# Two bottleneck layers on one core: the order of the four matmuls in a group of the projections and the last convolutions

## The chip, the core and the metric

The kernel runs on one core of one Trainium2 chip. A core has TensorE (matrix products, written to the PSUM memory), VectorE and ScalarE (elementwise work), GpSimd and SyncE (here mostly issuing DMAs), and 16 DMA engines. The metric is the device time of one execution in microseconds (us). A lower time is better.

## What is computed

Two layers on an input x of 16 images, 1024 channels, 32 x 32 pixels, all in fp32. The first is a bottleneck with local self-attention, the second a bottleneck with a 3x3 convolution:

```python
# layer 0
residual = x
h = relu(bn(conv1x1(x, w_conv1)))                 # 1024 -> 256 channels
q = relu(bn(conv1x1(h, wq))); k = relu(bn(conv1x1(h, wk))); v = bn(conv1x1(h, wv))
kp = unfold3x3(k) + (pos_h + pos_w)               # 32 heads of 8 channels, 9 taps
attn = softmax(einsum('bgdhw,bgdkhw->bgkhw', q, kp), over the 9 taps)
h = relu(bn(einsum('bgdkhw,bgkhw->bgdhw', unfold3x3(v), attn)))
x = relu(bn(conv1x1(h, w_conv3)) + residual)      # 256 -> 1024 channels
# layer 1
out = relu(bn(conv1x1(x, w1)))                    # 1024 -> 256
out = relu(bn(conv3x3(out, w2)))
x = relu(bn(conv1x1(out, w3)) + x)                # 256 -> 1024
```

## The kernel before

The channels are cut into blocks of 128 (P), so 1024 channels are NC = 8 blocks and 256 channels are NW = 2. An image has HW = 1024 pixels; a matmul of the program takes 512 of them, a half (`halves`, L308). A PSUM tile `ps` is 128 x 1024 fp32, two banks of 512 columns, one for each half; there are four such tiles, handed round.

The work of TensorE is a list of stages, one per image and kind, written out by hand (L975 to L979). `P3` stands for three stages of image 3, C, Q and V; letters stand for:

- C, the first convolution (`first_conv`, L1028): for each of 8 input blocks `reduce_part` (L352) adds four matmuls at L358 into two PSUM tiles. ScalarE then makes h, with one instruction for each of the two channel blocks (L1037).
- Q and V, the projections (`project`, L444). For each block of output channels, `conv` (L448) issues four matmuls at L454: two halves of the pixels by two input blocks of h. The order is k block 0, q block 0, q block 1, k block 1, then a product with the positions (L492), then v block 0 and v block 1. ScalarE reads each result (L466) once all four matmuls are done.
- F, the fused stage (`fused`, L1065). For each of 8 output blocks `Expand.products` (L386) issues four matmuls at L390 from the attention output a, and `reduce_part` takes the result at once into the second layer's first convolution (L358). The residual block s is put into the PSUM tile ahead by ScalarE (`seed`, L379 to L381), and `result` (L401, L417) reads the sum.
- W, the 3x3 convolution of four images in Winograd form (L771).
- U, the last 1x1 convolution (`last_sum`, L1106), again through `Expand.products`, from y.

The list puts a Q directly behind a C for thirteen images: 0 to 8, 10, 11, 13 and 14. Images 9, 12 and 15 have a U or a V in between or in front.

The attention itself (softmax over taps, weighted sums) is VectorE's, with two exps on ScalarE (L613). It takes q, k and v from DRAM in another layout and leaves the weighted sum `acc` (L631 to L651). A DMA stores that (L653), two DMAs fetch it back as the two channel blocks of a (L667), and ScalarE applies the norm and relu to each block (`finish_attended`, L670, instructions at L675).

[...] A planner in the program (`class Side`, L868) decides, while the program is built, between which steps of TensorE the pieces of attention and the exps are put, from fixed costs such as CHUNK = 3.43 (L436). DMAs are issued on three queues: loads of x, s and r and stores of results on GpSimd's, weights, the k and v stores and a on SyncE's, a few on ScalarE's.

The lines that matter are L388 to L397, L452 to L460, L356 to L364 (the inner order of the convolution into 256 channels, untouched), L381, L417, L466, L492, L1037 and L675.

Of the kernel before, what the change touches and what calls it, by code (L numbers as in the profile page):

```python
# [18 lines left out]
NW = WID // P  # L19
# [53 lines left out]
def sa_bottleneck_kernel(ctx: ExitStack, tc: tile.TileContext, x, w1t, wqkvt, w3t, u1t, u2t, u3t, params, out):  # L73
# [59 lines left out]
    def done_with(key):  # L133

        if last_use[key] == now[0]:
            more_weights()
# [3 lines left out]
    def col(name, j, n=1):  # L140
        return par[:, _COL[name] + j : _COL[name] + j + n]
# [160 lines left out]
    def inside(t, n):  # L302
        return t[:, n, 1 : 1 + H, 1 : 1 + W]

    def rows(ap):
        return ap.rearrange("p (r w) -> p r w", w=W)

    def halves(half):  # L308
        return slice(half * HALF, (half + 1) * HALF)
# [39 lines left out]
    def piece(name, half):  # L349
        return name, owner[now[0], name, half], half  # L350
# [20 lines left out]
    class Expand:  # L371
# [13 lines left out]

        def products(self, o):  # L386
            key = piece(self.name, o * 2 // NC)
            for half in range(2):  # L388
                for n in range(NW):
                    nc.tensor.matmul(  # L390
                        self.ahead[o][:, halves(half)],
                        pieces[key][:, n, o % (NC // 2) * P :][:, :P],
                        self.src[:, n, halves(half)],
                        start=False,
                        stop=(n == NW - 1),
                        skip_group_check=True,
                    )  # L397
            if o % (NC // 2) == NC // 2 - 1:
                done_with(key)
# [38 lines left out]
    def by_quarter(name, b, width, per):  # L438


        t = dram.tile([NJ, NW, P * per // HEAD_DIM, width], F32, tag=f"{name}{b}", name=name)
        return t.rearrange("j n c w -> n c j w"), t.rearrange("j n (g d) w -> (j n g) (d w)", d=per)

    def project(b):  # L444

        h = hidden.pop(b)

        def conv(which, n):  # L448
            ps = psum.tile([P, HW], F32, tag="ps", name="ps")
            name, at = ("wqk", which * WID) if which < 2 else ("wv", 0)  # L450
            key, at = piece(name, 0), at + n * P
            for half in range(2):  # L452
                for m in range(NW):
                    nc.tensor.matmul(  # L454
                        ps[:, halves(half)],
                        pieces[key][:, m, at : at + P],
                        h[:, m, halves(half)],
                        start=(m == 0),
                        stop=(m == NW - 1),
                    )  # L460
            if n == NW - 1 and which:
                done_with(key)
            return ps

        def norm(dst, src, name, n, func):
            nc.scalar.activation(  # L466
                dst, src, func,
                bias=col(f"L0_conv_{name}_b", n), scale=col(f"L0_conv_{name}_s", n),
            )

        def halo(name, which, func):

            room, backs[name] = by_quarter(name, b, HALO, HEAD_DIM)
            for n in range(NW):
                norm(inside(kp, n), rows(conv(which, n)), name, n, func)

                block = kp[:, n]
                nc.sync.dma_start(
                    room[n], AP(block.tensor, block.offset, [block.ap[0], [JROWS * PW, NJ], [1, HALO]])
                )  # L480
                yield CHUNK

        backs = relaid[b] = {}
        q = hpool.tile([P, NW, HW], F32, tag="h", name=f"q_{b}")
        room, backs["q"] = by_quarter("q", b, JPIX, HEAD_DIM)

        def positions():

            ps = psum.tile([P, HW], F32, tag="ps", name="ps")
            for half in range(2):  # L490
                for n in range(NW):
                    nc.tensor.matmul(  # L492
                        ps[n * G * NPOS : (n + 1) * G * NPOS, halves(half)],
                        pos[:, n].rearrange("p g t -> p (g t)"),
                        q[:, n, halves(half)],
                        start=True,
                        stop=True,
                    )
            by_offset = zpool.tile([P, HW], F32, tag="z", name="by_offset")
            nc.scalar.activation(by_offset, ps, AF.Identity)  # L500

            room, backs["pos"] = by_quarter("pos", b, JPIX, NPOS)
            by_offset = by_offset.rearrange("p (j w) -> p j w", j=NJ)
            for n in range(NW):
                nc.gpsimd.dma_start(room[n], by_offset[n * G * NPOS : (n + 1) * G * NPOS])

        k = halo("bnk", 1, RELU)
        yield next(k)
        for n in range(NW):
            norm(q[:, n, :], conv(0, n), "bnq", n, RELU)  # L510
            nc.gpsimd.dma_start(room[n], q[:, n, :].rearrange("p (j w) -> p j w", j=NJ))
            yield CHUNK
        yield next(k)
        positions()
        side.add(b)
        written.add(("qk", b))
        relay("qk", b)
        yield 2.5
        for n, cost in enumerate(halo("bnv", 2, AF.Identity)):
            if n:  # L520
                written.add(("v", b))
                relay("v", b)
            yield cost
# [11 lines left out]
    def relay(what, b):  # L535

        if not ((what, b) in written and (what, b) in room_for):
            return
        moved, backs = projected.setdefault(b, {}), relaid[b]
        if what == "qk":  # L540
            shapes = (("q", "qc", [HEAD_DIM, JPIX]), ("bnk", "bnk", [HEAD_DIM, HALO]), ("pos", "pc", [NPOS, JPIX]))
        else:
            shapes = (("bnv", "bnv", [HEAD_DIM, HALO]),)
        def move(name, tag, shape):
            t = apool.tile([P] + shape, F32, tag=tag, name=f"{tag}_{b}")
            nc.gpsimd.dma_start(t.rearrange("p d w -> p (d w)"), backs[name])
            moved[name] = t.rearrange("p d (r w) -> p d r w", w=PW) if shape[1] == HALO else t
            if len(moved) in (3, 4):
                come[what, b] = max(side.vector, side.tensor) if b else side.tensor

        for i, shape in enumerate(shapes):
            if b < 2 or i == 0:
                move(*shape)
            else:

                moves.append((side.tensor + GAP * i, lambda shape=shape: move(*shape)))
# [190 lines left out]
    def winograd_conv(b):  # L747
# [93 lines left out]
        for one, two in ROWS:  # L841
            for part in range(3):
                for i in (one, two):
                    products(i, part)
                    if part == 0:
                        copied(i, ones, 2.0)
                    elif part == 1:
                        copied(i, twos, 1.0)
                        side.other(along(i))
                        if i == 0:  # L850

                            middle(3, 0, 4.0)
                            side.other(6.0)
                    else:
                        side.other(last(i))
                    yield CHUNK + 0.3
# [379 lines left out]
```

## Time and profile before

| | before |
|---|---|
| median of 8 runs | 2415.78 us (2413.3 to 2418.47) |
| profiled execution, its own time | 2415.5 us |
| span of the profiled execution | 2413.7 us |
| TensorE matmul busy | 2382.8 us (99%), 6144 records |
| TensorE weight load busy | 1149.5 us (48%), 6144 records |
| VectorE busy | 2080.1 us (86%) |
| ScalarE busy | 919.4 us (38%) |
| GpSimd busy | 466.1 us (19%) |
| DMA | 691.04 MB, mean 286 GB/s |
| mean granted TensorE clock | 0.998 |

The profile is of one execution. Its span is counted from the first to the last instruction, and the execution's own time is 1.8 us more. "Busy" of the matmuls counts overlapping records once, and since a matmul's end overlaps the next one's start, the pitch from one start to the next says more than the duration of one. The profile's lines name the source line (L390), the engine (PE is the matmul, PEld the weight load, DVE is VectorE, ACT is ScalarE), the operation, output and inputs, the shape, and how often (x1024). What stands in brackets, or behind the last bar, is the time for which the engine had been idle before, and what ended that wait.

### The profile page before, as it was taken

The page shows a single profiled execution, that of the slowest core. Times are in us where ns is not written, and L with a number is a line of the kernel's source. Part 1 is how long each engine was busy: PE and PEld are TensorE (multiplying, and loading weights), DVE is VectorE, ACT ScalarE, POOL GpSimd, SP SyncE. Part 2 cuts the span into 40 slices and gives each one's busy share as a digit, 9 for nine tenths or more (in the row PEclk, how much of TensorE's full clock was granted, in tenths as well). Part 3 has the DMA queues.
Part 4 walks back from the last instruction along what each step waited for, and adds up shares of the span by engine and source line. Part 5 has one row for each costly group of instructions (what it writes and reads, how often), then busy time and mean ns, then how long its engine had stood idle before and what let it go on. Part 6 is the DMA issues. An engine that isn't in the chain of part 4 may idle for free.

```text
span 2413.7 us, 18460 instructions
## 1 busy us (share of the span) xinstructions
PE 2382.8 (99%) x6144; PEld 1149.5 (48%) x6144; DVE 2080.1 (86%) x1648; ACT 919.4 (38%) x889; POOL 466.1 (19%) x854
## 2 busy tenths in 40 slices
PE   8999999999999999999999999999999999989999
PEld 3444444444476444444476444444466444434844
DVE  4899999999999999998999999989989999873700
ACT  3323241323122574432122574334122553344265
POOL 2111111111111232111111232111111221112132
PEclk9999999999999999999999999999999999999999
DMA  9968685888798897777898997787798986788886
GB/s 357 365 209 309 246 297 211 262 294 264 267 327 273 322 395 290 237 262 242 240 312 294 298 409 273 251 283 261 243 321 302 319 327 227 241 283 271 321 297 252
DMA packets 296126, 691.04 MB, mean 286 GB/s; under 512 B 20064, under 2 KB 166496, under 8 KB 287584
## 3 DMA queue, kind: packets, MB, share of 16 engines
q0 software_dynamic: 119024, 471.40, 54.1%
q1 hardware_dynamic: 175568, 213.97, 28.0%
q10 hardware_dynamic: 1440, 4.51, 0.5%
q8 instruction: 49, 0.80, 0.1%
q14 instruction: 45, 0.37, 0.0%
HBM read 416.09 MB, written 273.70 MB: 286 GB/s over the span
## 4 chain that ended last, share of the span: by engine, by line
PE 84%; DVE 5%; DMA 4%; issue 4%; ACT 1%; POOL 1%; SPq 0%; POOLq 0%; ACTq 0%; DVEq 0%
PE ps L358 34%; PE ps L390 29%; PE ps L454 11%; PE ps L771 9%; DVE acc L631 2%; DVE acc L649 1%; PE ps L492 1%; DMA a<-a 1%; DMA U<-uw 1%; POOL out_dram L418 1%; DMA a<-acc 1%; POOL r L340 1%; ACT h L1037 1%; DMA uw<-u 0%; DMA v<-v 0%
## 5 line engine op out<-in xcount | busy, mean ns | idle before, releaser
L390 PE MATMUL ps<-a,w 128*128 128x512 f32 x1024 | 461.1, 595 | 7.2 <-ACT a L675 7.2
L358 PE MATMUL ps<-result,u 128*128 128x512 f32 x1024 | 458.4, 592 | 2.0 <-ACT result L417 2.0
L358 PE MATMUL ps<-x,w 128*128 128x512 f32 x1024 | 445.1, 595 | 6.5 <-DMA x<-in_x_dram 6.5
L390 PE MATMUL ps<-y,u 128*128 128x512 f32 x1024 | 441.2, 592 | 1.0 <-ACT ps L381 1.0
L631 DVE TENSOR_TENSOR acc<-e,bnv 128x2048 f32<-128x2048 f32 x144 | 327.5, 2283 | 36.6 <-ACT e L613 33.6
L574 DVE TENSOR_TENSOR prod<-qc,bnk 128x2048 f32<-128x2048 f32 x144 | 324.0, 2287 | 1.7
L417 ACT ACTIVATE result<-ps,par 128x1024 f32<-128x1024 f32 x128 | 142.5, 1113 | 463.2 <-PE ps L390 394.7
L390 PEld LDWEIGHTS ps<-a,w 128*128 128x128 f32 x1024 | 195.3, 191 | 255.0 <-issue 242.5
L358 PEld LDWEIGHTS ps<-x,w 128*128 128x128 f32 x1024 | 195.6, 191 | 252.8 <-issue 252.8
L358 PEld LDWEIGHTS ps<-result,u 128*128 128x128 f32 x1024 | 194.2, 190 | 248.3 <-issue 237.5
L390 PEld LDWEIGHTS ps<-y,u 128*128 128x128 f32 x1024 | 194.5, 190 | 245.9 <-issue 240.8
L649 DVE TENSOR_TENSOR acc<-acc 128x2048 f32<-128x2048 f32 x128 | 293.4, 2292 | 4.4
L454 PE MATMUL ps<-h,wqk 128*128 128x512 f32 x512 | 225.8, 595 | 5.7 <-ACT h L1037 5.7
L417 ACT ACTIVATE result<-ps,bn_sh 128x1024 f32<-128x1024 f32 x127 | 141.2, 1112 | 137.8 <-PE ps L390 137.5
L418 POOL DMA_DIRECT2D r<-result x128 | 68.8, 537 | 634.8 <-ACT result L417 619.3
L579 DVE TENSOR_TENSOR prod<-prod 128x2048 f32<-128x2048 f32 (+1 forms) x80 | 166.2, 2078 | 2.5
L454 PEld LDWEIGHTS ps<-h,wqk 128*128 128x128 f32 x512 | 96.2, 190 | 132.7 <-issue 110.0
L1037 ACT ACTIVATE h<-ps,par 128x1024 f32<-128x1024 f32 x32 | 38.6, 1205 | 288.1 <-PE ps L358 288.1
L381 ACT ACTIVATE ps<-r 128x1024 f32<-128x1024 f32 x128 | 130.4, 1020 | 26.3 <-DMA r<-r 18.8
L466 ACT ACTIVATE kp<-ps,par 128x1024 f32<-128x1024 f32 x64 | 77.4, 1210 | 160.2 <-PE ps L454 123.9
L381 ACT ACTIVATE ps<-s 128x1024 f32<-128x1024 f32 x128 | 131.2, 1025 | 2.5
L340 POOL DMA_DIRECT2D x<-in_x_dram x120 | 63.8, 532 | 299.9 <-PE ps L358 230.2
(317 smaller groups left out, 2296.1 us busy)
## 6 DMA issues: line engine op xcount, KB each, us to landing
s<-in_x_dram POOLq DMA_DIRECT2D x128, 512.0 KB, 6.3
r<-result POOLq DMA_DIRECT2D x128, 512.0 KB, 4.0
r<-r POOLq DMA_DIRECT2D x128, 512.0 KB, 6.3
out_dram<-result POOLq DMA_DIRECT2D x127, 512.0 KB, 6.1
x<-in_x_dram POOLq DMA_DIRECT2D x120, 512.0 KB, 5.2
v<-v SPq DMA_DIRECT2D x96, 408.0 KB, 4.7
U<-uw SPq DMA_DIRECT2D x72, 512.0 KB, 4.3
bnk<-kp SPq DMA_DIRECT2D x32, 680.0 KB, 7.7
```

The lines of the kernel that those rows point to most:

```text
L340: (nc.scalar if kind == "x" and b == 0 else nc.gpsimd).dma_start(t, src)
L358: nc.tensor.matmul(ps[n][:, halves(half)], wt[:, c % (NC // 2), n * P : (n + 1) * P], src[:, halves(half)], start=(c == first), stop=(c == ...
L381: nc.scalar.activation(ps, loaded.pop((self.kind, self.b, o)), AF.Identity)
L390: nc.tensor.matmul(self.ahead[o][:, halves(half)], pieces[key][:, n, o % (NC // 2) * P :][:, :P], self.src[:, n, halves(half)], start=Fals ...
L417: nc.scalar.activation(to_, ps, RELU, bias=self.shift(o), scale=1.0)
L418: nc.gpsimd.dma_start(to, t)
L454: nc.tensor.matmul(ps[:, halves(half)], pieces[key][:, m, at : at + P], h[:, m, halves(half)], start=(m == 0), stop=(m == NW - 1),)
L574: nc.vector.tensor_tensor(by_row(t[:, two]), by_row(qc), kc[:, :, i : i + JROWS, j : j + W], ALU.mult)
L579: nc.vector.tensor_add(u[:, :, 0:4], u[:, :, 0:4], u[:, :, 4:8])
L631: nc.vector.tensor_tensor(by_row(dst), rows(e[:, k, :]).unsqueeze(1).to_broadcast([P, HEAD_DIM, JROWS, W]), vc[:, :, i : i + JROWS, j : j ...
L649: nc.vector.tensor_add(acc, acc, t)
L771: nc.tensor.matmul(acc[i][:, at, :, n, :], pieces[key][:, m, at, n * P : (n + 1) * P], v[:, at, :, m * (TILES + TR) :][:, :, :TILES], star ...
```

## The change

In two places the two inner loops change places. `n` and `m` count the two blocks of input channels (the rows over which the products are summed), `half` the two halves of the pixels.

```diff
--- before.py
+++ after.py
@@ -385,8 +385,8 @@
         def products(self, o):
             key = piece(self.name, o * 2 // NC)
-            for half in range(2):
-                for n in range(NW):
+            for n in range(NW):
+                for half in range(2):
                     nc.tensor.matmul(
                         self.ahead[o][:, halves(half)],
                         pieces[key][:, n, o % (NC // 2) * P :][:, :P],
@@ -449,8 +449,8 @@
             ps = psum.tile([P, HW], F32, tag="ps", name="ps")
             name, at = ("wqk", which * WID) if which < 2 else ("wv", 0)
             key, at = piece(name, 0), at + n * P
-            for half in range(2):
-                for m in range(NW):
+            for m in range(NW):
+                for half in range(2):
                     nc.tensor.matmul(
                         ps[:, halves(half)],
                         pieces[key][:, m, at : at + P],
```

Before, a group of four was half 0 with blocks 0 and 1, then half 1 with blocks 0 and 1. After, it is block 0 with halves 0 and 1, then block 1 with halves 0 and 1. Two matmuls in a row then have the same weights and write different banks. The rest of the program text is the same.

## The prediction

> **What bounds the kernel now.** I read, in order, the page's busy table, the waits of TensorE, the costliest groups, and then the timeline at each wait. TensorE is 99% busy by the page (VectorE 86%), and the granted clock is full in nearly every slice. Its waits in the whole span, from the view that names who waited for whom, are few:
>
> ```profile
> PE ps L390 <- ACT a L675: 7.2, 2, 3.7
> PE ps L358 <- DMA x<-in_x_dram: 6.5, 1, 6.5
> PE ps L454 <- ACT h L1037: 5.7, 13, 0.4
> ```
>
> (total us, times, longest). The third row is the change's business, and the first in part. The groups show what a matmul costs when nothing is waited for:
>
> ```profile
> L390 PE MATMUL ps<-a,w 128*128 128x512 f32 x1024 | 461.1, 595 | 7.2 <-ACT a L675 7.2
> L358 PE MATMUL ps<-x,w 128*128 128x512 f32 x1024 | 445.1, 595 | 6.5 <-DMA x<-in_x_dram 6.5
> L358 PEld LDWEIGHTS ps<-x,w 128*128 128x128 f32 x1024 | 195.6, 191 | 252.8 <-issue 252.8
> ```
>
> Each `nc.tensor.matmul` is two records here: the first convolution issues 16 images x 8 blocks x 4 = 512, and the row counts 1024. The pitch of the records, from the chain of waits in order of time (start, us, what):
>
> ```profile
> 113.37 27.48 PE ps L358 x64
> 782.30 27.47 PE ps L390 x64
> 809.76 13.73 PE ps L454 x32
> 1163.32 13.14 PE ps L454 x30
> ```
>
> 27.48/64, 27.47/64 and 13.73/32 are all 0.429 us. So one program matmul is 0.858 us, in all three loops. TensorE is the bound, at a pitch that the order inside a group of four does not set; only its waits can be won.
>
> **The change, part by part.** It touches 2048 + 768 = 2816 records (L390 and L454). Nothing is added or removed: same matmuls, operands, helpers' order, DMAs and queues. Inside each group of four, the second and third matmul swap. [...]
>
> *Steady state: 0.* The new order keeps one stationary operand for two matmuls and alternates PSUM banks; that is exactly the inner order of L358 (its n outside, half inside). [...] L358 already repeats its weights, and shows 1024 loads for 1024 matmul records at the same 0.429 pitch. I take the row: no load goes, and a load would be worth nothing anyway, since it lies beside the matmul before it. [...] The distance from one accumulation to the next in the same bank becomes one matmul; it was none in L390 before, and is three or more in L358. Both ends run at 0.429, so I take 0 for what lies between.
>
> *The start of thirteen projections.* Where a projection follows a first convolution at once, its input h comes in two ACT instructions, one for each channel block. The timeline at image 1 (second is the duration):
>
> ```profile
> 88.33 1.20 ACT L1037 ACTIVATE h<-ps,par 128x1024 f32<-128x1024 f32 x1 [5.08 <-PE ps L358]
> ...
> 89.84 1.02 PE L454 MATMUL ps<-h,wqk 128*128 128x512 f32 x2
> 90.04 1.20 ACT L1037 ACTIVATE h<-ps,par 128x1024 f32<-128x1024 f32 x1 [0.51 <-PE ps L358]
> 91.30 1.98 PE L454 MATMUL ps<-h,wqk 128*128 128x512 f32 x4 [0.44 <-ACT h L1037]
> ```
>
> Block 0 is ready before the convolution ends; block 1 only at 90.04 + 1.20 = 91.24. The first matmul starts at 89.84, before the second ACT even begins, so the wait is on the block and not on the whole of h. The second matmul (half 0, block 1) could start at 89.84 + 0.858 = 90.70, and starts at 91.30: 0.60 lost. After such a stop the next record takes 0.697 instead of 0.592 (the maximum in the L454 rows), 0.105 more. Sum **0.705**. A cross-check: a projection of 32 records without a stop runs from 809.60 to 823.43 (13.83); this one runs from 89.84 to 104.37 (14.53), 0.70 longer.
>
> After the change the second matmul reads block 0 again. Block 1 is first read by the third, due at 89.84 + 1.716 = 91.56, 0.26 after the release at 91.30. The weight load that carries the wait would be due about 0.43 earlier, at 91.13, and so starts 0.17 late. That this is free is seen at image 0: its first L454 load starts at 36.79 where the regular step from 36.20 gives 36.63, and its matmul is at 37.05 all the same, one step after the last. So each stop goes whole, and nothing is late in its place: 13 x 0.705 = 9.2 us on TensorE.
>
> *Which of these reach the end.* The other engines' programs keep their order, so a gain is lost only where TensorE waits next for something that did not move. Image 0 (stop at 38.5): at 53.54 TensorE waits for q, behind an ACT that waits for a DMA begun at 40.94, after h; lost. Images 2 and 3 (142.1, 193.0): at 223.95 the fused stage waits 1.49 us for a result that sits behind a of image 0. That chain is VectorE's, from 144.48 on, started by an exp that follows the h of image 2 and not the stop. Lost: 1.4 us. The other **ten** (91.3, 301.3, 408.0, 458.9, 564.6, 670.4, 1163.3, 1214.2, 1597.0, 1757.7) lie in the printed chain as "h, then PE L454 x30", like the row at 1163.32 above. Behind them TensorE waits for nothing of more than 0.75 us until 2129. VectorE has finished each image's attention 37 us or more before its fused stage from image 1 to 14, and its last piece starts at 2067.05, after waiting 8.72 us for an exp behind ACT work that follows TensorE. So VectorE moves along. 10 x 0.705 = **7.05 us**. Bounds: 9.2 if all thirteen count, 3.5 if half of the ten are absorbed.
>
> *The fused stage of image 15.* Here a's two blocks arrive apart, by the timeline of TensorE:
>
> ```profile
> 2129.27 2.08 PE L390 MATMUL ps<-a,w 128*128 128x512 f32 x2 [3.50 <-ACT a L675]
> 2135.06 6.51 PE L390 MATMUL ps<-a,w 128*128 128x512 f32 x10 [3.71 <-ACT a L675]
> ```
>
> One matmul is done before the second block; with the change it is two, so two records fewer remain after 2135.06: 2 x 0.429 = **0.86 us**. The clock is half here (0.50 in each of the stretches from 2129.0 to 2139.0, 0.99 after), so this is counted at the pitch that follows. The trace cannot tell whether the busier stretch brings the clock back one window (about 3.4 us) sooner: upper end 0.86 + 1.7 = 2.6, lower end 0.86. I take the lower, since the 2129.00 to 2132.40 stretch was 2.08 us busy already and the clock stayed.
>
> In all other fused and last stages a, or y, is ready long before; there the swap does nothing: 0. The groups that wait for a seed wait at their first matmul in either order: 0.
>
> **Sum.** 7.05 + 0.86 = 7.9. The profiled execution took 2415.5 us (span 2413.7, 1.8 around it), 0.3 under the median shown: 2415.5 - 7.9 = 2407.6; against the median 2407.9. I say 2407.7.
>
> **Rivals.**
> - *The clock returns a window sooner* at 2132 or 2136: 2407.7 - 1.7 = 2406.0. For: more work in that window. Against: 2.3 us of idleness remain there. Chance 0.10.
> - *VectorE is the true bound* (86%, nines in most slices), and the gains only lengthen the wait for a at 2129: what stays is 0.86 and 2414.6. Also here: the waits do not shorten because they were tied to all of h. Against: the first matmul's start before the second ACT, and the 8.72 us of VectorE idleness ahead of its last piece. Chance 0.08.
> - *Half is absorbed*, by a longer landing on the path: a of image 15 took 15.25 us from issue to landing, and a weight piece U of the last Winograd stage 13.70 against a median of 4.3. 3.5 + 0.86 gives 2411.2; with one further 9.4 us landing it is 2417. Chance 0.13.
> - *Slower: the banks.* If returning to a bank after one other matmul breaks the stream, each of the 1408 program matmuls pays. It outweighs the gain from 7.9/1408 = 5.6 ns each; at the 0.105 us that a restarted stream pays above it is +148, hence 2556. L358's four banks speak against, and that the distance of one is nowhere in the trace, for. Chance 0.03.
> - The forecast: 0.66.
>
> 0.2% of this time, about what a measurement can tell from no change, is 4.8 us. Faster by more: 0.66 + 0.10 + 0.03 of the half case = 0.79; within: 0.17; slower: 0.04 (the banks, and 0.01 of late landings). The range 2404 to 2412.5 takes in the sooner clock, all thirteen stops, and half of them lost.
>
> **What would show it.** Right: the row "PE ps L454 <- ACT h L1037" is gone or near zero; all projections run at 32 records in 13.7; L390 and L454 keep a count of two loads and two matmuls per program matmul and 0.429; the waits at 53.5 and 223.9 are longer by 0.7 and 1.4; four records instead of two stand before the second a. Wrong: a pitch other than 0.429 in L390 or L454, the wait at 2129 longer by some 7 us, or fewer loads.

## The result and the profile after

| | before | after |
|---|---|---|
| median | 2415.98 us (32 runs, 2411.33 to 2422.71) | 2409.76 us (12 runs, 2405.85 to 2413.35) |
| ratio | | 0.9974, 95% interval 0.9967 to 0.9982 |
| profiled execution, own time | 2415.5 us | 2413.8 us |
| span | 2413.7 us | 2412.1 us |
| TensorE matmul busy, records | 2382.8 us, 6144 | 2382.2 us, 6144 |
| weight loads | 6144 | 6144 |
| mean granted clock | 0.998 | 0.996 |

The changed kernel is 6.2 us faster, with an interval of 4.3 to 8.0; 7.9 had been forecast. The profiled execution of the changed kernel is the longest of its thirteen, so its span is not the measure. What follows reads it in stretches.

The waits of TensorE after (who waited for whom: total us, times, longest):

```profile
PE ps L390 <- ACT a L675: 6.4, 2, 4.1
PE ps L358 <- DMA x<-in_x_dram: 6.2, 1, 6.2
PE ps L358 <- ACT result L417: 4.2, 1, 4.2
PE ps L492 <- ACT q L466: 2.5, 1, 2.5
PE ps L454 <- ACT by_offset L500: 2.3, 1, 2.3
```

The row of thirteen waits for h is gone altogether. Three others have grown. Before, they were:

```profile
PE ps L358 <- ACT result L417: 2.0, 2, 1.5
PE ps L492 <- ACT q L466: 0.9, 1, 0.9
PE ps L454 <- ACT by_offset L500: 0.3, 1, 0.3
```

The costliest groups after:

```profile
L390 PE MATMUL ps<-a,w 128*128 128x512 f32 x1024 | 462.7, 597 | 6.4 <-ACT a L675 6.4
L390 PEld LDWEIGHTS ps<-a,w 128*128 128x128 f32 x1024 | 195.9, 192 | 255.3 <-issue 243.3
L454 PE MATMUL ps<-h,wqk 128*128 128x512 f32 x512 | 222.3, 592 | 0.0
```

There is still one weight load for each matmul record, although every second matmul of the program in these two loops now has the weights of the one before it. The last of these rows was, before:

```profile
L454 PE MATMUL ps<-h,wqk 128*128 128x512 f32 x512 | 225.8, 595 | 5.7 <-ACT h L1037 5.7
```

So it fell by 3.5 us, with nothing idle before it. Image 1 again, in the timeline after, and, in the chain of waits, the projection that stood at 1163.32 before:

```profile
89.10 1.20 ACT L1037 ACTIVATE h<-ps,par 128x1024 f32<-128x1024 f32 x1 [5.85 <-PE ps L358]
90.61 3.60 PE L454 MATMUL ps<-h,wqk 128*128 128x512 f32 x8
90.82 1.21 ACT L1037 ACTIVATE h<-ps,par 128x1024 f32<-128x1024 f32 x1 [0.51 <-PE ps L358]
```

```profile
1162.53 13.73 PE ps L454 x32
```

The projection now runs on while the second ACT writes block 1. At 1162.53 it is one unbroken piece of 32 records at 13.73/32 = 0.429 us, where before the chain went over ACT and then 30 records.

**Where the gain went.** TensorE has the same 6144 records in the same stages in every kernel here, so the starts of the same record can be compared. Record 761, counted from 1, opens the second reduction (L358) of image 1's fused stage, some 7 us behind the wait near 330 us. Record 5371 lies just before the fused stage of image 15. Worked out from the traces of all profiled kernels that belong here (us; the labels are those of the experiments below):

| kernel | start of record 761 | 761 to 5371 | 5371 to the last |
|---|---|---|---|
| before | 337.9 | 1785.14 | 285.5 |
| e3, new order where nothing waits | 336.4 | 1785.14 | 284.6 |
| e5, last convolutions alone | 341.3 | 1785.14 | 286.2 |
| e1, images 0 to 4 alone | 339.0 | 1785.13 | 282.5 |
| e2, eight later images alone | 342.2 | 1779.50 | 286.4 |
| after | 341.2 | 1779.50 | 286.2 |
| e8, after once more | 349.1 | 1779.52 | 280.9 |
| e12, after once more | 340.2 | 1783.45 | 284.7 |
| e10, before with one store moved | 334.9 | 1785.16 | 281.6 |
| e9, after with that store moved | 335.1 | 1779.81 | 284.5 |
| e11, e9 once more | 336.9 | 1780.91 | 285.1 |

The middle column settles the main point. With the eight later stops it is 1785.13 to 1785.16 in each of these profiles, without them 1779.50 to 1779.52 in three: 5.64 us, or 0.705 for each stop. In the other three TensorE waits besides in a Winograd stage: e9 and e11 have 0.3 and 1.4 us more, e12 3.95, from one wait of 2.2 us for a weight piece U at 699 and half clock behind it. The first column shows no gain from the five early stops, the last none from image 15; both scatter by several us. They also say little about the medians: the profiled executions of after, e2, e5, e8 and e12 are the longest of their series, that of e10 the shortest.

### The profile page after: what moved, and what is told of

It is laid out like the page before. It is cut to its first block, busy times and chain, and to the rows that moved or that the text cites. A ratio compares the mean times of both kernels' runs of the same rounds, so it can differ in the third digit from the quotient of the medians.

```text
span 2412.1 us, 18460 instructions
## 1 busy us (share of the span) xinstructions
PE 2382.2 (99%) x6144; PEld 1151.7 (48%) x6144; DVE 2080.1 (86%) x1648; ACT 919.3 (38%) x889; POOL 466.1 (19%) x854
## 4 chain that ended last, share of the span: by engine, by line
PE 82%; DVE 9%; issue 4%; DMA 3%; POOL 1%; ACT 1%; POOLq 0%; ACTq 0%; SPq 0%; DVEq 0%
PE ps L358 32%; PE ps L390 29%; PE ps L454 11%; PE ps L771 10%; DVE acc L631 3%; DVE acc L649 2%; DVE prod L574 1%; PE ps L492 1%; POOL out_dram L418 1%; DMA a<-a 1%; DVE prod L579 1%; POOL r L340 1%; DMA bnk<-kp 1%; DMA uw<-u 0%; DMA U<-uw 0%
## 5 line engine op out<-in xcount | busy, mean ns | idle before, releaser
L358 PE MATMUL ps<-result,u 128*128 128x512 f32 x1024 | 459.6, 594 | 4.2 <-ACT result L417 4.2
L358 PE MATMUL ps<-x,w 128*128 128x512 f32 x1024 | 443.7, 594 | 6.2 <-DMA x<-in_x_dram 6.2
L358 PEld LDWEIGHTS ps<-x,w 128*128 128x128 f32 x1024 | 195.1, 191 | 251.5 <-issue 251.0
L358 PEld LDWEIGHTS ps<-result,u 128*128 128x128 f32 x1024 | 194.9, 190 | 250.8 <-issue 238.1
L1037 ACT ACTIVATE h<-ps,par 128x1024 f32<-128x1024 f32 x32 | 38.5, 1205 | 287.1 <-PE ps L358 287.1
L466 ACT ACTIVATE kp<-ps,par 128x1024 f32<-128x1024 f32 x64 | 77.4, 1209 | 151.2 <-PE ps L454 114.6
```

Of the source, the lines that this page charges most:

```text
L358: nc.tensor.matmul(ps[n][:, halves(half)], wt[:, c % (NC // 2), n * P : (n + 1) * P], src[:, halves(half)], start=(c == first), stop=(c == ...
```

## The experiments

Each was run in turn with the kernel before on the same chip. Unless said otherwise, an edit is to the kernel before.

**e1: the new order in the early images alone.**

```diff
-            for half in range(2):
-                for m in range(NW):
+            order = [(m, half) for m in range(NW) for half in range(2)]
+            if not (b in (0, 1, 2, 3, 4)):
+                order.sort(key=lambda at: at[1])
+            for m, half in order:
```

> The new order in the projections of images 0 to 4 alone; all else as before. All five stops at the first projection go, 3.5 us on TensorE. Theory A (gains before 330 us are lost, since what TensorE waits for at 330 hangs on VectorE, which did not move): 0 us in the median, ratio 1.0000, and the first matmul of the fused stage of image 1 that waits for a result (330.7 us before) comes within 1.5 us of its old time. Theory B (as the prediction has it, the stops of images 1 and 4 count): -1.4 us, 0.9994. Theory C (every stop counts): -3.5 us, 0.9985. If longer waits cost clock windows besides, A gives up to +3 us.

Measured: 2416.76 against 2415.0 us, ratio 1.0008 (1.0000 to 1.0016). The trace shows where the gain went in that execution. By 301 us TensorE was 3.6 us ahead of the kernel before (1.6 of it from a quicker start of that execution), and at the next wait 3.2 of them went. ScalarE, then SyncE's queue, in the timeline of e1 (two lines inserted above shift its numbers: L468 is L466 of before, L480 is L478, L738 is L736):

```profile
310.79 1.21 ACT L468 ACTIVATE kp<-ps,par 128x1024 f32<-128x1024 f32 x1 [2.23 <-PE ps L456]
...
328.04 1.21 ACT L468 ACTIVATE kp<-ps,par 128x1024 f32<-128x1024 f32 x1 [9.14 <-DMA bnk<-kp]
329.15 1.10 ACT L417 ACTIVATE result<-ps,par 128x1024 f32<-128x1024 f32 x1
```

```profile
313.74 1.40 SPq L738 DMA_DIRECT2D v<-v  x2
315.19 0.60 SPq L130 DMA_DIRECT2D w<-ws  x1
315.89 0.41 SPq L480 DMA_DIRECT2D bnk<-kp  x1
```

Block 1 of k is written by 312.0, but its store is issued only at 315.89, behind a store of Winograd data (v) on the same queue that waits for VectorE. The store lands at 328.0. Only then may ScalarE write v into the same buffer, and the result that TensorE waits for stands behind that write:

```profile
330.30 5.40 PE L358 MATMUL ps<-result,u 128*128 128x512 f32 x8 [3.76 <-ACT result L417]
```

In the kernel before the same place was:

```profile
330.70 3.93 PE L358 MATMUL ps<-result,u 128*128 128x512 f32 x8 [0.48 <-ACT result L417]
```

What TensorE waits for here hangs on VectorE and a landing, so a TensorE that comes earlier waits longer. The landing counts too: in e1 the store took 12.1 us from its issue until ScalarE went on, in the kernel before 10.9. The eight records then take 5.40 us instead of 3.93, since the clock is half from 330.5 to 333.9. Theory A, with its clock window, is the one that fits; B and C lie outside the interval of the median, which leaves no gain.

**e2: the eight later images alone.** The same edit with the images 5, 6, 7, 8, 10, 11, 13 and 14.

> The new order in the projections of images 5, 6, 7, 8, 10, 11, 13 and 14 alone; all else as before. Eight stops of 0.705 us go, all behind 330 us. Theories A, B and C: -5.6 us, 2410.3, ratio 0.9977. If VectorE were the bound behind 330 too: within 1 us of before.

Measured: 2410.84 us, 0.9984 (0.9976 to 0.9992), that is 1.9 to 5.8 us. The 5.6 lies at the upper end, and the trace shows 5.64 in the middle stretch to the hundredth. This profile also has a wait of 2.9 us at 333.5 with a half-clock window, though its code is that of before up to there. With the early stops in place that wait was 0.5 us in two profiles (before and e3), 2.9 and 4.1 in two others (e2 and e5, the longest executions of their series) and not there in e4; without them it was 3.3 to 4.2 in four (after, e1, e8, e12).

**e3: the new order wherever nothing waits.** The edit of e1 with `b in (9, 12, 15) or (which, n) != (1, 0)`, and the like in `products` with all but the fused stage of image 15.

> The new order wherever nothing is waited for: all projection groups but the first (k, block 0) of the thirteen images behind a first convolution, and all groups of the last convolutions but the fused stage of image 15. If the order costs nothing in itself: ratio 1.0000, pitch 0.429 us in L390 and L454, and the row of waits for h unchanged at 13. If the alternation of banks or the repeated weights were worth something, 2816 records less the excepted ones would show it: 1 ns a record is 2.6 us.

Measured: 2415.15 us, 0.9999 (0.9992 to 1.0006); the thirteen waits for h are there, and the middle stretch is 1785.14, as before. The order in itself is worth nothing, neither by its weights nor by its banks.

**e4: the stop made longer.** The late block first, in the first group of the thirteen:

```diff
+            late = (which, n) == (1, 0) and b not in (9, 12, 15)
             for half in range(2):
-                for m in range(NW):
+                for m in reversed(range(NW)) if late else range(NW):
...
-                        start=(m == 0),
-                        stop=(m == NW - 1),
+                        start=(m == (NW - 1 if late else 0)),
+                        stop=(m == (0 if late else NW - 1)),
```

> As before, but in the first projection group of the thirteen images the late block of h comes first (in both halves), so that the first matmul and not the second waits for it. The stop grows from 0.60 + 0.105 to 1.46 + 0.105 us, by 0.86. If eight to ten stops lie on the path to the end: +6.9 to +8.6 us, ratio 1.003. If all thirteen count: +11.2. If VectorE hides them: +1 or less.

Measured: 2425.1 us, 1.0041 (1.0028 to 1.0054), +10.1 (6.8 to 13.0). Its waits row (one line inserted above shifts the numbers):

```profile
PE ps L455 <- ACT h L1038: 16.8, 13, 1.3
```

Thirteen waits of 1.3 us. The middle stretch is 1791.98, +6.84 for eight stops, 0.855 each as computed. The rest of the +10.1 is not placed: the stretches outside the middle scatter too much, and the interval holds both eight stops and thirteen. At the eight, TensorE's time is the kernel's time, in both directions.

**e5: the last convolutions alone.** The first hunk of the change.

> The new order in the last convolutions alone (L390), projections as before. Only the fused stage of image 15 can gain: four records instead of two before the late block of a, 0.86 us, ratio 0.9996 (to -2.6 us, 0.9989, if the clock comes back a window sooner). If the longer first burst makes the clock no better and the wait takes a further window, 0 to +1 us. The thirteen waits for h stay.

Measured: 2414.56 us, 0.9995 (0.9987 to 1.0003): cannot be told from nothing, nor from the 0.86. In its trace the move happened and did not pay. In the changed kernel's it is the same:

```profile
2127.53 3.78 PE L390 MATMUL ps<-a,w 128*128 128x512 f32 x4 [4.09 <-ACT a L675]
2133.65 7.74 PE L390 MATMUL ps<-a,w 128*128 128x512 f32 x11 [2.33 <-ACT a L675]
```

Four records stand before the late block, as forecast. But the half clock holds until 2139.2, and did until 2139.0 before (13.7 us of it in the changed kernel's profile, 10.2 in the first), and how long these waits are differs by us from profile to profile (from record 5371 to the last: 281.6 to 287.1 in all profiles with the old order at this place, 280.9 to 286.2 with the new one).

**e6 and e7: all stores of k and v on ScalarE's queue.** In `halo`, on the changed kernel (e6) and on the one before (e7):

```diff
-                nc.sync.dma_start(
+                nc.scalar.dma_start(
                     room[n], AP(block.tensor, block.offset, [block.ap[0], [JROWS * PW, NJ], [1, HALO]])
```

> The changed kernel, and the stores of k and v (L478) issued by ScalarE's DMA queue instead of SyncE's, where the store of k's block 1 of image 4 stood behind a store of Winograd data that waits for VectorE (issued at 317.64, its data ready at 313.76). Theory A (the wait at 330 eats the early gains through that queue): the store goes some 3.5 us sooner, the wait of 4.2 us for the result at 332.5 falls under 1.5, no half-clock window follows it, and the median falls by 2 to 5 us under the changed kernel, to 2405 to 2408. If the landing is bound by the DMA engines and not by the issue: no change against the changed kernel. If ScalarE pays for 64 issues of about 0.4 us where TensorE waits for it: slower by a few us.

> The kernel before, with the stores of k and v on ScalarE's queue as in e6. Theory A: with that wait out of the way the order of the matmuls is worth more than before: this minus e6 is 7 to 9 us (8 stops of 0.705 behind 330, 0.7 to 2.1 ahead of it, 0.86 at image 15), and this one is within 3 us of the kernel before, since its wait at 330 was 0.5 us. If the early gains are lost elsewhere: the difference stays near 6.

Measured: 2426.55 us, 1.0043 (1.0030 to 1.0056), and 2427.11 us, 1.0045 (1.0033 to 1.0057). Both miss what was expected by far, and so does their difference: 0.6 us, where 7 to 9, or else 6, had been expected. The wait near 330 did go (in e6 the store was issued at 318.98, right behind its activation of 317.74). Others came or grew elsewhere, in e6 these:

```profile
PE ps L390 <- ACT ps L381: 5.9, 4, 2.6
PE ps L454 <- ACT by_offset L500: 5.3, 1, 5.3
PE ps L358 <- ACT result L417: 4.4, 1, 4.4
```

In two of the three ScalarE's own order shows. At by_offset ScalarE now issues the store before it (0.37 us, and 0.44 of waiting for its own write); the longer part of that wait is that the two blocks of a landed some 2.6 us later than in the changed kernel, and why was not tried. The wait for a result is at 614; on ScalarE that result (612.95) stands behind exps, the first of which had waited 12.30 us for VectorE. It is in e6 and not in e7, and with the half clock behind it puts e6 back by 7.1 us there, although each stop is still gone at its place, for 0.7 us. So in these two kernels the order does not show in the time: what was won at the stops was lost at a wait that came in one profile and not in the other.

**e8: the changed kernel again.**

> The changed kernel once more, for a second profile beside the others on one chip. All theories: ratio 0.9974 within its interval. Theory A: no wait for h, a wait for the first result near 330 again longer than the 0.5 us of before, and the eight stops behind it worth 5.6 us in the positions of TensorE's records; whether half-clock windows follow the waits at 54 and at 330 varies from run to run.

Measured: 2408.96 us, 0.9975 (0.9969 to 0.9982), 22 runs. The wait for a result was there again (3.9 near 330, 5.0 in two), and the middle stretch was 1779.52. One thing missed: there was a wait for h, of 1.2 us at 38.8. It stands before the first matmul of image 0's projection, that is, it is for the early block, so the order has no part in it. With a wait of 4.8 us for q at 60.15 it makes this profile's start the latest of the table.

**e9 and e10: one store moved.** On the changed kernel (e9) and on the one before (e10):

```diff
-                nc.sync.dma_start(
+                (nc.scalar if (name, n, b) == ("bnk", 1, 4) else nc.sync).dma_start(
```

> The changed kernel with one DMA moved: the store of k's block 1 of image 4 goes on ScalarE's queue, all 63 others stay on SyncE's. Theory A: it is issued right after its data (about 313 and not 317), the wait for the first result near 330 (4.2, 3.8 and 3.9 us in the three profiles with the early stops gone) falls under 1 us with no half-clock window of 1.4 us behind it, and the median falls 2 to 5 us under the changed kernel: 2404 to 2407, ratio to before 0.9955 to 0.9967. Theory D (the DMA engines are full there and the store lands late whatever the queue): as the changed kernel, 0.9975.

> The kernel before with that same one store on ScalarE's queue. Theory A: the wait at 330, 0.5 us in one profile of that code and 2.9 and 4.1 in two others, goes; 1 to 4 us under the kernel before. The order of the matmuls is then worth 7 to 8 us (e9 against this): 5.6 behind 330 and 1.4 ahead of it, and what image 15 gives. Theory D: as before, 1.0000, and the difference stays at 6.

Measured: e9 2406.85 us, 0.9966 (0.9954 to 0.9979); e10 2416.2 us, 1.0003 (0.9994 to 1.0011). The rows did what theory A says. In e9 the store goes at 313.85, and TensorE walks from the last convolution into the reduction without a wait:

```profile
321.33 7.03 PE L390 MATMUL ps<-a,w 128*128 128x512 f32 x16
328.19 3.60 PE L358 MATMUL ps<-result,u 128*128 128x512 f32 x8
```

Record 761 came at 335.1 and 334.9, earlier than in all the others. But e10's median did not fall, and its profile is its shortest execution, 7.6 us under that median. The medians of e9 and e10 are 9.4 us apart, where 7 to 8 had been expected, or 6; with five runs of e9 this does not tell one from the other.

**e11 and e12: e9 and the changed kernel once more, side by side.**

> e9 once more, beside the changed kernel on the same chip, to settle whether the moved store is worth anything in the median. Theory A: 2 to 4 us under e12, ratio to before 0.996 to 0.9967. Theory D: the same as e12 within 1 us.

> The changed kernel a third time, beside e11. All theories: ratio 0.9974 within its interval; in the profile no wait for h, and a wait of 3 to 5 us for the first result near 330.

Measured: e11 2409.32 us, 0.9974 (0.9964 to 0.9984); e12 2408.77 us, 0.9976 (0.9964 to 0.9988). Theory D's number: the moved store is worth nothing that can be measured, although it takes the wait at 330 away (record 761 at 336.9, no wait for a result in its list). So that wait explains the early loss in the profiles in which it stands; that it does so in the median was not shown, and what else holds the first 330 us is open. In the profile of e11 the wait just ahead of it, at 212, was 3.5 us with a half-clock window, where e12 had 1.1 and none. No version that beats the changed kernel was found.

## Why the prediction was right

*The bound and the steady state: right.* TensorE, at 0.429 us a record in either order (13.73 us for 32 records of a projection before and after; the middle stretch of e3 is that of before, 1785.14). There are 6144 loads before and after, and no half clock came with the alternating banks (0.998 granted in the mean before, 0.996 after, 0.998 in e3; in the profiles of before and after the half clock between 15 and 2300 us lies at waits or right behind them). Each record has a load of its own in every order here, so what one load for two matmuls would be worth was not tried.

*The stop of 0.705 us: right.* Thirteen of thirteen are gone in the changed kernel's profile, 0.705 each for the eight that the middle stretch measures; its lengthening by e4 was right too.

*Which stops reach the end: partly wrong.* The prediction's step was "the other ten lie in the printed chain" and "behind them TensorE waits for nothing of more than 0.75 us until 2129". The wait at 330.7, small in that profile, was passed over. It does not follow TensorE: it hangs on a store behind VectorE's on SyncE's queue, and in the profile of e1 it took what the stop at 301.3 and those ahead of it had won. None of the five early stops is seen in the median of e1. Eight count, 5.64 us, in place of ten and 7.05. Of the two waits that were to grow, the one for q at 53.5 grew by 1.6 us instead of 0.7, and the one at 223.9 went, since TensorE was already held 2.1 us longer at 212, by by_offset, which stands behind a of image 0 on ScalarE.

*Image 15: the step failed in its result.* The two records more before the late block are there, but the 0.86 us for them is seen in no median and no stretch. The wait around it varies by more.

*The sum.* The measured 4.3 to 8.0 holds both 5.6 and the forecast's 7.9, so the time alone does not show that two of the ten stops and image 15 are missing; the median's 6.2 lies nearer to eight stops. The parts run alone (e1 +1.8, e2 -4.2, e5 -0.6) add up to about -3, with some 1.9 us of uncertainty in each; that they come to less than the whole is within what such a sum can be off, and is left open.

*The rivals.* VectorE is not the bound of the middle stretch. In the profiles with a wait near 330 it is part of what holds TensorE there; the rival had placed its effect at 2129. The banks cost nothing (e3: 0.9999 of the time before). Whether the clock returns sooner at image 15 is not told apart: its half clock lasts 3.4 to 13.7 us in the profiles with the new order there, 6.8 to 13.7 in those with the old. One figure of the half case is a slip: 2417 is the forecast of 2407.6 with a 9.4 us landing; on top of 2411.2 it would be 2420.6.

## What to carry to other kernels

When an input arrives in pieces, one behind the other (here two of 1.20 us from ScalarE), order the consumer so that everything that the first piece allows comes before the first use of the second; two matmuls of cover (1.7 us) hid the rest of a 1.2 us activation thirteen times, at no cost. Before counting such gains to the end, look for the next wait of the bound engine even where it is short: what ended it tells whether it moves along, and a short one in one profile may be long in the next (near 330, 0.5 us in the profile of before, 2.9 in that of e2, whose code is the same up to there). Comparing the start of the same record in two traces, stretch by stretch, resolved hundredths of a us where the medians resolved about two us.

## What was not expected of the hardware

A short wait of TensorE can cost more than itself. With some came half clock, in the profiles of before and after for 3.41 to 13.65 us at a time, in which the records ran at 0.85 us instead of 0.43. The changed kernel's stretches near 330 (busy time of TensorE, its weight loads, VectorE, ScalarE and GpSimd, then the clock granted to TensorE, DMA share, GB/s):

```profile
324.00:328.00 4.00, 4.00 (x11) 1.56 (x9) 3.93 (x4) 0.00 (x0) 0.00 (x0) 1.00 1.05 335
328.00:332.00 4.00, 0.31 (x1) 0.00 (x0) 3.50 (x4) 1.72 (x2) 0.00 (x0) 1.00 1.15 325
332.00:336.00 4.00, 3.46 (x6) 1.39 (x7) 3.93 (x5) 3.36 (x4) 1.97 (x4) 0.70 1.08 323
336.00:340.00 4.00, 4.00 (x10) 1.81 (x9) 4.00 (x2) 0.00 (x0) 0.18 (x1) 0.88 1.09 272
```

The wait fills most of 328 to 332 at full clock; the half clock falls on the work behind it and costs some 1.5 us more (5.40 us for the eight records instead of 3.93). The kernel before had no such window at 330 in its profile, where its wait was 0.5 us.

Not every wait had half clock with it. In the changed kernel's profile a wait of 2.47 us for q (50.19 to 52.66) had 3.41 us of half clock behind it, from 53.68, and one of 2.34 us for by_offset (210.27 to 212.61) had none, with 1.00 granted from 205 to 218. In the profile of the kernel before a wait of 1.49 us for a result (222.46 to 223.95) had none, and the two for a, of 3.50 and 3.71 us, came with 10.24 us of it, from 2128.79. So the length of a wait alone does not tell what it costs; what decides was not shown.
